# Small products on parts of the TensorE array: row tiles of 64 for the products with T and T^2, column tiles of 64 for the logits

## The chip, the cores and the metric

The kernel runs on one core of one Trainium2 chip. The metric is the device time of one execution in microseconds (us). Most executions of one kernel agree within 0.3%. Engines are named as in the profile: PE is TensorE's matmul stream, PEld its weight loads, DVE is VectorE, ACT is ScalarE, POOL is GpSimd. L880 is line 880 of that kernel's source, so the line numbers of one operation differ between kernels.

## The reference, cut to what matters

128 graphs of 64 nodes with 512 features pass four layers. Two of them are touched. All is fp32.

```python
# layer 2: attention inside a graph
weight = jnp.einsum('bqd,bkd->bqk', query, keyt)          # logits, 64 x 64 per graph
weight = adj * jnp.exp(weight)
...
# layer 3: three hops with a transition matrix T (64 x 64 per graph)
H = jnp.zeros(...)
Xk = X
for k in range(3):
    H = H + Xk @ Wk[k] + bk[k]
    Xk = jnp.einsum('bij,bjd->bid', transition, Xk)        # so X, T X and T^2 X are needed
```

## The kernel before

Two graphs make one tile of 128 tokens, and four tiles one group; there are 16 groups. Products inside a graph are done for both graphs of a tile at once, with a 128 x 128 matrix that is zero outside the two 64 x 64 blocks. So half of the multiplications are by zeros (T, T^2) or their results are thrown away (logits).

```python
# layer 3, per tile t: h (tokens x features) stationary, [T^t | (T^2)^t] moving, 256 columns
for q in range(2):
    pq = Buf("ps")
    def lm(h=h, pq=pq, t=t, q=q):
        for c in range(2):
            cc = 2 * q + c
            nc.tensor.matmul(pq.t[:, c * 2 * P:(c + 1) * 2 * P], h.t[:, cc * P:(cc + 1) * P],
                             tt.t[:, t].rearrange("p j k -> p (j k)"), start=True, stop=True)
    pe(c_mm(256, 2), lm, [h, (tt, 0), (tt, 1)], [pq])
    act(0.59, ...)                                         # copy out of PSUM
# layer 2, per emission of a quarter of the query
for o in range(2):
    for t in range(2):
        nc.tensor.matmul(quad(pl)[:, 2 * j + t, :], hT.t[:, 2 * i + o, tok(2 * j + t)], q.t[:, o, tok(t)], ...)
```

The kernel does not issue its operations in program order: a list scheduler written into it orders them by assumed costs and priorities and hands out the buffers; `pe(cost, ...)` is one indivisible operation for it. The large products are Strassen products (one helper line, L555), and they make most of the work.

## Time and profile before

The time was 2607.03 us (median of 3 runs). TensorE is busy 2562 us of the 2607. Of its 12058 matmul records, 512 are the products with T and T^2 (L880) and 512 the logits (L796); the prediction below shows their lines and works out what one costs. It calls this cost a slot: the time from the start of one matmul to the start of the next in an unbroken stream. The mean duration of a matmul on the page is longer, since matmuls overlap.

### The profile page before, as it was taken

The page shows a single profiled execution, that of the slowest core. Times are in us where ns is not written, and L with a number is a line of the kernel's source. Part 1 is how long each engine was busy: PE and PEld are TensorE (multiplying, and loading weights), DVE is VectorE, ACT ScalarE, POOL GpSimd, SP SyncE. Part 2 cuts the span into 40 slices and gives each one's busy share as a digit, 9 for nine tenths or more (in the row PEclk, how much of TensorE's full clock was granted, in tenths as well). Part 3 has the DMA queues.
Part 4 walks back from the last instruction along what each step waited for, and adds up shares of the span by engine and source line. Part 5 has one row for each costly group of instructions (what it writes and reads, how often), then busy time and mean ns, then how long its engine had stood idle before and what let it go on. Part 6 is the DMA issues. An engine that isn't in the chain of part 4 may idle for free.

```text
span 2606.9 us, 32072 instructions
## 1 busy us (share of the span) xinstructions
PE 2562.2 (98%) x12058; PEld 2047.3 (79%) x12058; DVE 1771.4 (68%) x4064; ACT 783.4 (30%) x1370; POOL 710.4 (27%) x843
## 2 busy tenths in 40 slices
PE   8999999999999999999879999999999999999999
PEld 4667777777777777767768888888888888888887
DVE  8887788788787888778675545555455564555653
ACT  2343333343333433433222212222122221222211
POOL 3323334332233433333211212122221222211220
PEclk9999999999999999999989999999999999999999
DMA  4031001011001111101220000100001000010000
GB/s 162 21 110 37 17 25 37 33 37 37 21 21 37 33 37 37 37 7 34 65 89 21 33 30 28 37 25 29 33 25 37 29 29 33 21 37 25 25 21 25
DMA packets 53355, 96.18 MB, mean 37 GB/s; under 512 B 7760, under 2 KB 7760, under 8 KB 53200
## 3 DMA queue, kind: packets, MB, share of 16 engines
q1 hardware_dynamic: 53200, 94.14, 10.8%
q8 instruction: 94, 1.54, 0.2%
q14 instruction: 61, 0.50, 0.1%
HBM read 59.52 MB, written 34.60 MB: 36 GB/s over the span
## 4 chain that ended last, share of the span: by engine, by line
PE 95%; DVE 4%; issue 0%; ACT 0%; POOL 0%; DVEq 0%; ACTq 0%; POOLq 0%
PE ps L555 58%; PE ps L773 15%; PE ps L880 4%; PE ps L502 4%; PE ps L826 2%; PE ps L796 2%; PE ps L687 2%; PE ps L675 2%; PE ps L745 1%; PE ps L871 1%; DVE st L482 1%; DVE s_s_vu_tt L547 1%; PE ps L861 1%; PE ps L709 1%; PE ps L446 1%; PE ps L592 1%
## 5 line engine op out<-in xcount | busy, mean ns | idle before, releaser
L555 PE MATMUL ps<-wb_mem,rT_a 128*128 128x256 f32 x2056 | 476.9, 380 | 1.4 <-DVE u L527 0.8
L485 POOL TENSOR_TENSOR rs<-ve,mhalf 128x1 f32<-128x1 f32 x320 | 208.1, 653 | 937.4 <-DVE ve L484 896.7
L555 PEld LDWEIGHTS ps<-wb_mem,rT_a 128*128 128x128 f32 x2056 | 386.2, 190 | 67.4 <-issue 11.2
L493 ACT ACTIVATE h<-x,nm,rs 128x512 f32<-128x512 f32 x256 | 206.6, 815 | 359.3 <-DVE nm L492 269.8
L555 PE MATMUL ps<-wb_mem,s_s_vu_tt 128*128 128x256 f32 x1152 | 276.4, 379 | 0.1
L555 PE MATMUL ps<-wb_mem,tmp_s 128*128 128x256 f32 x1152 | 263.9, 379 | 0.0
L555 PEld LDWEIGHTS ps<-wb_mem,s_s_vu_tt 128*128 128x128 f32 x1152 | 215.6, 190 | 40.7 <-issue 7.5
L555 PE MATMUL ps<-wb_mem,mT_a 128*128 128x256 f32 x1016 | 242.9, 379 | 0.0
L555 PE MATMUL ps<-wa_mem,mT_a 128*128 128x512 f32 x512 | 241.3, 596 | 0.0
L555 PEld LDWEIGHTS ps<-wb_mem,tmp_s 128*128 128x128 f32 x1152 | 215.6, 190 | 27.5
L482 DVE BATCH_NORM_STATS2 st<-x 128x6 f32<-128x512 f32 x256 | 174.4, 686 | 62.7 <-DMA x<-xm 61.2
L555 PEld LDWEIGHTS ps<-wb_mem,mT_a 128*128 128x128 f32 x1016 | 190.0, 190 | 34.0 <-issue 7.7
L583 POOL TENSOR_TENSOR u<-u,bk_b 128x256 f32<-128x256 f32 x96 | 68.3, 725 | 472.9 <-DVE u L525 347.4
L555 PE MATMUL ps<-wa_mem,s_s_vu_tt 128*128 128x512 f32 x384 | 178.3, 594 | 5.5 <-DVE s_s_vu_tt L547 5.5
L555 PEld LDWEIGHTS ps<-wa_mem,mT_a 128*128 128x128 f32 x512 | 95.9, 191 | 86.5 <-issue 82.7
L527 DVE TENSOR_TENSOR u<-ps,u 128x512 f32<-128x512 f32 (+1 forms) x160 | 84.7, 529 | 115.6 <-PE ps L555 90.5
L502 PEld LDWEIGHTS ps<-bd,h 128*128 128x128 f32 x1024 | 130.2, 195 | 32.7 <-issue 18.7
L585 DVE TENSOR_TENSOR o<-ps,u 128x256 f32<-128x256 f32 x96 | 40.7, 424 | 153.5 <-PE ps L555 149.7
L504 ACT COPY mT_a<-ps 128x512 f32<-128x512 f32 x128 | 74.7, 584 | 232.7 <-PE ps L502 160.5
L726 POOL TENSOR_TENSOR x<-x,u 128x256 f32<-128x256 f32 x96 | 70.0, 742 | 259.2 <-DVE u L525 197.4
L502 PE MATMUL ps<-bd,h 128*128 128x128 f32 x1024 | 133.2, 279 | 6.9 <-ACT h L493 4.3
L555 PEld LDWEIGHTS ps<-wa_mem,s_s_vu_tt 128*128 128x128 f32 x384 | 71.9, 190 | 86.1 <-issue 68.6
(185 smaller groups left out, 4304.6 us busy)
## 6 DMA issues: line engine op xcount, KB each, us to landing
x<-in_x_dram SPq DMA_DIRECT2D x64, 256.0 KB, 2.7
xm<-x SPq DMA_DIRECT2D x64, 256.0 KB, 2.0
x<-xm SPq DMA_DIRECT2D x64, 256.0 KB, 2.6
out_dram<-x SPq DMA_DIRECT2D x64, 256.0 KB, 2.0
adj<-in_adj_dram SPq DMA_DIRECT2D x32, 256.0 KB, 2.6
wb_mem<-in_Wk_dram SPq DMA_DIRECT2D x6, 512.0 KB, 7.1
wa_mem<-in_W1T_dram SPq DMA_DIRECT2D x2, 1024.0 KB, 8.2
wb_mem<-in_W2T_dram SPq DMA_DIRECT2D x4, 512.0 KB, 6.2
```

Of the source, the lines that this page charges most:

```text
L482: dve(0.69, lambda i=i: nc.vector.bn_stats(st.t[:, i, :], src(i)), [r[i]], [(st, i)])
L485: pool(0.57, lambda: nc.gpsimd.tensor_tensor(rs.t, ve.t, mhalf, ALU.pow), [ve], [rs])
L493: act(0.82, lambda: nc.scalar.activation(h.t, xx.t, AF.Relu, bias=nm.t, scale=rs.t), [xx, nm, rs], [h])
L502: nc.tensor.matmul(quad(p)[:, c, :], h.t[:, c * P:(c + 1) * P], rhs(), start=True, stop=True)
L504: act(0.59, lambda: nc.scalar.copy(m.t, quad(p)), [p], [m])
L527: dve(c_v(n), lambda: nc.vector.tensor_add(at(2)(), p4.t[:, :n], at(1)()), [p4, (U, 1)], [(U, 2)])
L555: nc.tensor.matmul(p.t[:, :n], lhs()[:, c, :], rhs(c), start=first and c == 0, stop=c == kc - 1, skip_group_check=True)
L583: pool(0.75, lambda: nc.gpsimd.tensor_add(U.t[:, iv], U.t[:, iu], row()[:, cols]), [u, krow], [v])
L675: nc.tensor.transpose(quad(pt)[:, c, :], z.t[:, j * D + c * P:j * D + (c + 1) * P], ident)
L726: pool(0.75, lambda: nc.gpsimd.tensor_add(xx.t[:, cols], xx.t[:, cols], U.t[:, iu]), [xx, u], [xx])
L773: nc.tensor.matmul(pair(p.t)[:, o, :], a, b, start=first and o == 0 and c == 0, stop=c == 1, skip_group_check=True)
L880: nc.tensor.matmul(pq.t[:, c * 2 * P:(c + 1) * 2 * P], h.t[:, cc * P:(cc + 1) * P], tt.t[:, t].rearrange("p j k -> p (j k)"), start=True, ...
```

## The change

The products with T and T^2 go graph by graph, on 64 of the array's 128 rows, with 128 moving columns instead of 256, alternating between the upper and the lower rows. The logits go graph by graph on 64 of its columns. How the array is cut up (whole, row halves or column halves) is called its mode below. The scheduler learns to hand out two buffers of one kind to one operation.

```diff
@@ logits, layer 2
-                        nc.tensor.matmul(quad(pl)[:, 2 * j + t, :], hT.t[:, 2 * i + o, tok(2 * j + t)], q.t[:, o, tok(t)],
-                                         start=first and o == 0 and t == 0, ...)
-            pe(c_mm(128, 4), mm, ...)
+                        for s in HALVES:
+                            at = lambda t: slice(t * P + s.start, t * P + s.stop)
+                            nc.tensor.matmul(quad(pl)[s, 2 * j + t, s], hT.t[:, 2 * i + o, at(2 * j + t)], q.t[:, o, at(t)],
+                                             start=first and o == 0 and t == 0, ...)
+            pe(c_mm(64, 4), mm, ...)
@@ products with T and T^2, layer 3 (the loop over q is gone, one operation per tile)
+                pq = [Buf("ps"), Buf("ps")]
+                def lm(h=h, pq=pq, t=t):
+                    for c in range(KD):
+                        for i, half in enumerate(HALVES):
+                            nc.tensor.matmul(quad(pq[i])[:, c, :], h.t[half, c * P:(c + 1) * P], tt.t[half, t, :, half],
+                                             start=True, stop=True)
+                pe(c_mm(128, KD), lm, [h, (tt, 0), (tt, 1)], pq)
+                for i, half in enumerate(HALVES):
+                    act(0.59, ...)                         # copy of that half's columns
+                step(0.9)
@@ cut: the scheduler counts the free buffers that an operation needs; the Strassen products wait for both copies
```

More of the change, by code (lines that the diff above doesn't have):

```diff
@@ L110, in run @@
                     t = max(o.ready, at[e])
+                    need = {}
                     for b in o.bufs:
                         if id(b) not in place:
-                            f = free[b.tag]
-                            t = max(t, min(f)[0]) if f else float("inf")
+                            need[b.tag] = need.get(b.tag, 0) + 1
+                    for tag, n in need.items():
+                        f = free[tag]
+                        t = max(t, (min(f) if n == 1 else sorted(f)[n - 1])[0] if len(f) >= n else float("inf"))
                     if t0 is None or (t, o.prio, o.seq) < (t0, pick.prio, pick.seq):
@@ L795, in mm @@
                     for t in range(2):
-                        nc.tensor.matmul(quad(pl)[:, 2 * j + t, :], hT.t[:, 2 * i + o, tok(2 * j + t)], q.t[:, o, tok(t)],
-                                         start=first and o == 0 and t == 0, stop=False, skip_group_check=True)
-            pe(c_mm(128, 4), mm, [*k[j], (q, 0), (q, 1)] if first else [*k[j], (q, 0), (q, 1), pl], [pl])
+                        for s in HALVES:
+                            at = lambda t: slice(t * P + s.start, t * P + s.stop)
+                            nc.tensor.matmul(quad(pl)[s, 2 * j + t, s], hT.t[:, 2 * i + o, at(2 * j + t)], q.t[:, o, at(t)],
+                                             start=first and o == 0 and t == 0, stop=False, skip_group_check=True)
+            pe(c_mm(64, 4), mm, [*k[j], (q, 0), (q, 1)] if first else [*k[j], (q, 0), (q, 1), pl], [pl])
             step(0.9)
@@ L873, in layer3 @@
                 act(0.59, lambda p=p, b=b: nc.scalar.copy(b.t[:, :KD, :], quad(p)), [p], [(b, 0)])
-                for q in range(2):
-                    pq = Buf("ps")
-                    def lm(h=h, pq=pq, t=t, q=q):
-                        for c in range(2):
-                            cc = 2 * q + c
-                            nc.tensor.matmul(pq.t[:, c * 2 * P:(c + 1) * 2 * P], h.t[:, cc * P:(cc + 1) * P],
-                                             tt.t[:, t].rearrange("p j k -> p (j k)"), start=True, stop=True)
-                    pe(c_mm(256, 2), lm, [h, (tt, 0), (tt, 1)], [pq])
-                    act(0.59, lambda pq=pq, b=b, q=q: nc.scalar.copy(
-                        b.t[:, KD:, :].rearrange("p (j c) k -> p c j k", j=2)[:, 2 * q:2 * q + 2],
-                        pq.t.rearrange("p (c j k) -> p c j k", c=2, j=2)), [pq], [(b, 1 + q)])
-                    step(0.9)
+                pq = [Buf("ps"), Buf("ps")]
[6 more added lines that the diff above has]
+                for i, half in enumerate(HALVES):
+                    act(0.59, lambda pq=pq, b=b, i=i, half=half: nc.scalar.copy(
+                        b.t[:, KD:, half].rearrange("p (j c) k -> p c j k", j=2),
+                        pq[i].t.rearrange("p (c j k) -> p c j k", c=KD, j=2)), [pq[i]], [(b, 1 + i)])
+                step(0.9)
                 step(0.45)
@@ L899, in layer3 @@
                 b = a3[t0 + i]
-                ak[i, 0] = [(b, 0), (b, 1)]
+                ak[i, 0] = [(b, 0), (b, 1), (b, 2)]
                 ak[i, 1] = [(b, 1), (b, 2)]
```

## The prediction

> **What bounds the kernel now.** I read the page's busy shares first, then the chain of waits, then the matmul groups kept apart by shape, and last the timeline around four places where the form of the matmul changes.
>
> ```profile
> PE 2562.2 (98%) x12058; PEld 2047.3 (79%) x12058; DVE 1771.4 (68%) x4064; ACT 783.4 (30%) x1370; POOL 710.4 (27%) x843
> ...
> PE 95%; DVE 4%; issue 0%; ACT 0%; POOL 0%; DVEq 0%; ACTq 0%; POOLq 0%
> ...
> L880 PE MATMUL ps<-s_s_vu_tt,h 128*128 128x256 f32 x512 | 120.5, 379 | 0.0
> ...
> L796 PE MATMUL ps<-y_qT,z_hT 128*128 128x128 f32 x512 | 67.4, 275 | 0.6 <-ACT y_qT L784 0.6
> ```
>
> TensorE is busy 98% of the span and makes 95% of the chain that ended last; the two groups that the change touches stood idle for 0.0 and 0.6 us in all. So the time is the sum of TensorE's slots, and whatever these groups gain or lose goes straight into the span. The mean durations (379 and 275 ns) are not the slots, since matmuls overlap; the slots come from start to start in the timeline:
>
> ```profile
> 1369.97 3.62 PE L880 MATMUL ps<-s_s_vu_tt,h 128*128 128x256 f32 x16
> 1373.43 2.75 PE L555 MATMUL ps<-wb_mem,rT_a 128*128 128x256 f32 x12
> ...
> 1293.46 1.05 PE L796 MATMUL ps<-y_qT,z_hT 128*128 128x128 f32 x8
> 1294.35 0.60 PE L773 MATMUL ps<-z_hT,wa_mem 128*128 128x256 f32 x2
> ...
> 2527.62 0.79 PE ps L613 x8
> ```
>
> Products with T and T^2: (1373.43 - 1369.97)/16 = 0.216 us an instruction, and 512 of them are 110.7 us. Logits: (1294.35 - 1293.46)/8 = 0.111 us, and 512 are 57 us. Every product in fp32 is two matmul instructions, each with its own weight load (256 products are 512 records). The last line, from the chain, is a matmul that streams a single column behind a load of 128 columns: 0.79/8 = 0.099 us a slot. So a load of 128 columns alone costs about 0.1 us, and a product with 128 moving columns, at 0.111, sits on that floor as well. A saving on moving columns below 128 is worth nothing unless the loads also get shorter or run side by side.
>
> **What the Trainium skill says.** "TensorEngine Tiling (Array Packing)", section "Key Properties", says that different tiles of the array can load weights and multiply in parallel, and that a change of tiling mode (not of tile) drains TensorE. The first half is what the change lives on; nothing in this trace shows it, since no two tiles are ever used side by side. The second half the trace does show. The setup has matmuls on 2 columns (L413) and 2 rows (L417, L418) between full-array ones:
>
> ```profile
> 36.38 1.02 PE L555 MATMUL ps<-wa_mem,s_s_vu_tt 128*128 128x512 f32 x2
> 37.34 0.59 PE L413 MATMUL ps<-wb_mem,gsc 128*2 128x512 f32 x1
> ...
> 45.55 0.27 PE L675 MATMUL ps<-ident,z_hT 128*128 128x128 f32 x1
> 45.76 1.12 PE L417 MATMUL ps<-o,tmp_s 2*128 2x512 f32 x2
> ...
> 46.72 1.02 PE L418 MATMUL ps<-o,tmp_s 2*128 2x512 f32 x2
> 47.67 0.44 PE L675 MATMUL ps<-ident,z_hT 128*128 128x128 f32 x2
> ```
>
> The line of L555 ends at 36.38 + 1.02 = 37.40, and L413 starts at 37.34, 0.06 to 0.07 before that end; L675 ends at 45.82 and L417 starts at 45.76; L418 ends at 47.74 and L675 starts at 47.67. Three times the next form begins just before the recorded end of the last one, as if it had waited for the array to run empty, whereas within one form a matmul starts a full drain earlier. Worked out: two slots of 512 columns (0.43 us each: L418's two matmuls start 46.72 and end 1.02 later, of which 0.59 is the last one) from 36.38 would have put L413 at 37.24, so it lost about 0.09 us; one slot of 0.11 (a transpose, 0.44 us for four in the chain) from 45.55 would have put L417 at 45.66, so 0.10. On top, the first weight load behind a switch is not hidden: L417's first matmul lasts 0.69 us where the later ones last 0.59, which is one load of 128 columns (0.10). A switch thus costs about 0.09 + 0.11 = 0.2 us before 128-column weights and, by the same estimate, 0.09 + 0.055 = 0.145 us before 64-column weights or a transpose (its load is short: 0.14 us of record against 0.19).
>
> "TensorE: Matmul & The Clock Gate", section "Measured speedup vs the span model", gives 3.07x for four row tiles and 2.38x for three column tiles at 512 moving columns. Those are long matmuls; it says nothing of 64 or 128 moving columns with a fresh load for each, in fp32, which is this case. The same page's section "LDWEIGHTS (loading the stationary operand)" has the load time go with the columns and not with the rows. The trace agrees for the columns (L413's loads of 2 columns last 0.085 us, those of 128 columns 0.19); for rows, the 2-row loads of L417 and L418 last 0.18, about as long as a load of 128 rows. So halving the rows of the T products does not shorten any load.
>
> **The change, part by part.**
>
> *Products with T and T^2 (64 tiles of 128 tokens, 16 groups of 4).* Removed: 4 products a tile at 256 moving columns, 8 instructions x 0.216 = 1.73 us. Added: 4 feature blocks x 2 graphs = 8 products on 64 rows, 128 moving columns, 16 instructions with 16 loads of 128 columns. If the two halves of the array work side by side, loads included, each pass takes 0.111 us per pair. The order is first half twice (two fp32 passes), second half twice, so with matmuls started in order the second half runs one slot behind: 9 slots x 0.111 = 1.0 us. Gain 0.73 x 64 = 47 us. Against it go the switches in and out of the mode, 0.2 + 0.2 us (0.145 for the way out where a transpose follows, say 0.37 for both). In the trace the L880 records come in 61 unbroken runs, 17 of which hold two whole tiles; a tile is now one operation, so I count about 50 blocks: 50 x 0.37 = 18.5 us. Net -28 us.
>
> *Logits (16 groups x 4 emissions).* Removed: 4 products of 128 x 128 with 128 moving columns, 8 x 0.111 = 0.89 us. Added: 8 products, 64 stationary and 64 moving columns, 16 instructions. Loads and streams are half as long, 0.056 us. Side by side: 9 x 0.056 = 0.50 us, gain 0.39 x 64 = 25 us. Switches: L796 stands in 63 separate runs between full-array matmuls, each with 0.145 in and 0.2 out: 22 us. Net -3 us even if all goes well.
>
> *Moved.* Copies of the products out of PSUM stay 2 x 512 elements a tile on ScalarE (0.585 us each, an engine at 30%), but a tile now needs two PSUM buffers at once and both copies before the next Strassen product may start. With TensorE fed from two groups of graphs at once, I expect that wait to be filled. The list scheduler gets other costs and one priority step fewer per tile, so the order in layers 2 and 3 shifts; TensorE idles about 45 us in all now (2606.9 - 2562.2), 10 of them in one wait at the start of the second phase, so that is worth a few us either way.
>
> Sum if tiles pair in both parts: -28 - 3 = -31 us, 2576.
>
> **Rivals.**
>
> *The loads do not pair.* One load at a time over the whole array would make the T products 16 x 0.111 = 1.78 us a tile, 0.05 more than now, plus switches: +3 + 18.5 = +21 us. The same for logits: 16 x 0.056 = 0.9 us, no gain, plus switches, +21 us. Both together 2649. For it: in the present trace loads never overlap in effect (the 0.1 us slot of one-column matmuls). Against it: the skill's statement of independent tiles; and the author's cost model counts pairs. I give pairing of row tiles two chances in three.
>
> *Issue becomes the bound.* The logits would need 32 instructions (loads and matmuls) in 0.5 us, 16 ns each. Nothing in the trace runs that fast: eight one-column matmuls with eight loads take 0.79 us, 49 ns per instruction, though the loads explain that. If 25 to 30 ns per instruction is the floor, an estimate from nothing better than that line, the logits take 0.8 to 0.96 us: no gain, and the 22 us of switches are paid, +15 to +27. The row tiles (32 instructions in 1.0 us) would just fit. I hold it as likely as the good case. Rows paired and columns not: -28 + 20 = -8, 2599.
>
> *No switch cost.* If a tile of 64 switches without draining, all of 47 + 25 = 72 us is gained, 2535, faster by 2.8%. The switches in setup speak against it.
>
> *ScalarE or PSUM becomes a wait.* With ScalarE at 30% and DVE near 55% in the second half this can only cost at the last group, where little else runs; 1 to 3 us.
>
> **Range and chances.** The four combinations are 2576 (both pair), 2599 (rows only), 2625 (columns only) and 2649 (neither). With two in three for rows and one in two for columns the mean is 0.33 x 2576 + 0.33 x 2599 + 0.17 x 2625 + 0.17 x 2649 = about 2604, and the middle of the weight lies at the first two; I lean to the median side of that, since the change was written by someone who counts on pairs, and choose 2595. An order that shifts by a few us widens the ends: 2562 to 2642. Over 2% faster means below 2555, which needs cheaper switches than the trace shows; over 2% slower means above 2659, which needs loads that are not even prefetched inside a tile mode. I give each 8%.
>
> **What would show it right or wrong.** Right: matmuls of 64*128 whose starts, over a tile, come to about 1.0 us for 16, with a gap of some 0.2 us ahead of the first one and of the matmul behind the last; the logits' 16 of 128*64 in 0.5 us (pairing) or 0.9 (not); TensorE still at 97% or more. The first phase (layers 0 and 1, up to about 1230 us) should be unchanged. Wrong: 16 row-tile instructions in 1.7 us or more; no gap at the switches; loads that start only after the matmul before them has ended; or new idle time of TensorE behind ScalarE's copies.

## The result, and the profile after

The changed kernel took 2574.98 us (median of 4 runs), against 2606.89 us for the kernel before beside it: 31.9 us less. The ratio is 0.9877, with a 95% interval of 0.986 to 0.9894. The time lies inside the range that was predicted, but the gain is 2.7 times the 12 us of the point.

The busy shares of the changed kernel, on the page:

```profile
PE 2519.7 (98%) x13082; PEld 1988.6 (77%) x13082; DVE 1798.6 (70%) x4064; ACT 786.3 (31%) x1370; POOL 713.8 (28%) x843
```

TensorE has 1024 more matmuls, and its busy time is 42.5 us shorter, while the span is 32 us shorter. It is still the bound, and it idles about 10 us more (55 us against 45). The groups by shape (engine, line, operation, output and inputs, shapes, count; busy us, mean ns; idle before):

```profile
L885 PE MATMUL ps<-s_s_vu_tt,h 64*128 64x128 f32 x1024 | 69.3, 286 | 9.4 <-ACT s_s_vu_tt L868 9.4
...
L801 PE MATMUL ps<-y_qT,z_hT 128*64 128x64 f32 x1024 | 43.8, 228 | 0.6 <-ACT y_qT L787 0.6
```

The busy time is the time in which at least one matmul of the group runs: 69.3 us where L880 had 120.5, and 43.8 where L796 had 67.4, for twice as many matmuls. Both kinds of tile do run side by side. And there is a wait that L880 didn't have, 9.4 us behind L868, the copy of T^2 out of PSUM.

The chain of waits of the changed kernel (start, length, what) shows a block of logits with its neighbours, and in a later stretch the new wait:

```profile
1454.52 1.73 PE ps L776 x8
1456.25 0.61 PE ps L801 x16
1456.86 1.92 PE ps L776 x8
...
1512.06 0.97 PE ps L866 x8
1513.03 0.02 issue
1513.06 0.59 ACT s_s_vu_tt L868
1513.65 0.04 issue
1513.69 2.98 PE ps L885 x48
```

The chain of the kernel before had the same neighbours around its logits:

```profile
2507.71 0.89 PE ps L796 x8
2508.60 2.59 PE ps L555 x12
2511.19 0.89 PE ps L796 x8
2512.08 8.63 PE ps L773 x40
```

A block of logits went from 0.89 to 0.61 us. But the eight projection matmuls behind it take 1.92 us where the same eight take 1.73 behind other products on the whole array: 0.19 us, the way out of the mode. So a block nets 0.89 - 0.61 - 0.19 = 0.09 us, and 63 blocks some 6 us.

Inside the blocks the starts say how full the array is. In a block of one tile's row tiles two matmuls start 6 or 7 ns apart, and from the second pair on the next two follow 112 ns later; in a block of logits it is 6 or 7 ns and 58 ns. Eight slots, in both, and the second slot comes late behind the first load. The timeline of one block of row tiles, matmuls alone:

```profile
1479.69 1.16 PE L885 MATMUL ps<-s_s_vu_tt,h 64*128 64x128 f32 x16
1480.79 0.70 PE L831 MATMUL ps<-s_s_vu_tt,bd 128*128 128x512 f32 x1
```

The 16 matmuls occupy 1.10 us from first start to the next operation's start, where two of the 0.86 us halves of L880 stood. The first matmul of L831 lasts 0.70 us, as L417's 0.69 did in the prediction; later ones of that shape last 0.59. That is the load that isn't hidden.

### The profile page after: what moved, and what is told of

The parts are those of the page before. It is cut to its first block, busy times and chain, and to the rows that moved or that the text cites. A ratio compares the mean times of both kernels' runs of the same rounds, so it can differ in the third digit from the quotient of the medians.

```text
span 2574.9 us, 34142 instructions
## 1 busy us (share of the span) xinstructions
PE 2519.7 (98%) x13082; PEld 1988.6 (77%) x13082; DVE 1798.6 (70%) x4064; ACT 786.3 (31%) x1370; POOL 713.8 (28%) x843
## 4 chain that ended last, share of the span: by engine, by line
PE 95%; DVE 4%; ACT 1%; issue 0%; POOL 0%; DVEq 0%; ACTq 0%; POOLq 0%
PE ps L558 59%; PE ps L776 15%; PE ps L505 4%; PE ps L885 3%; PE ps L831 2%; PE ps L690 2%; PE ps L678 2%; PE ps L801 1%; PE ps L876 1%; PE ps L748 1%; DVE st L485 1%; DVE s_s_vu_tt L550 1%; PE ps L866 1%; PE ps L595 1%; PE ps L712 1%; PE ps L449 1%
## 5 line engine op out<-in xcount | busy, mean ns | idle before, releaser
L488 POOL TENSOR_TENSOR rs<-ve,mhalf 128x1 f32<-128x1 f32 x320 | 195.6, 614 | 1136.5 <-DVE ve L487 1065.1
L586 POOL TENSOR_TENSOR u<-u,bk_b 128x256 f32<-128x256 f32 x96 | 83.8, 892 | 207.5 <-DVE u L530 98.6
L526 ACT COPY u<-ps 128x512 f32<-128x512 f32 (+1 forms) x160 | 73.3, 458 | 221.7 <-PE ps L558 120.9
L505 PE MATMUL ps<-bd,h 128*128 128x128 f32 x1024 | 133.2, 279 | 7.0 <-ACT h L496 4.3
```

The lines of the kernel that those rows point to most:

```text
L488: pool(0.57, lambda: nc.gpsimd.tensor_tensor(rs.t, ve.t, mhalf, ALU.pow), [ve], [rs])
L505: nc.tensor.matmul(quad(p)[:, c, :], h.t[:, c * P:(c + 1) * P], rhs(), start=True, stop=True)
L526: act(n / 1200 + 0.17, lambda: nc.scalar.copy(at(0)(), p1.t[:, :n]), [p1], [(U, 0)])
L586: pool(0.75, lambda: nc.gpsimd.tensor_add(U.t[:, iv], U.t[:, iu], row()[:, cols]), [u, krow], [v])
```

## The experiments

The theory after the result: (1) both kinds of tile pair fully, 8 slots a block; (2) every change of mode costs about 0.09 us before the first matmul starts, as if the array had to run empty, and one unhidden load (0.10 us for 128 columns, 0.05 for 64); (3) the new order of instructions takes part of the gain back, by the wait behind the copy of T^2. The rivals: the order makes the gain rather than costing it; the logits carry as much as the T products; switches are cheap.

### One part at a time

**e1_rows_only.** The changed kernel with the logits of the kernel before (the diff of the logits above, undone). The scheduler's assumed cost is the same for both forms, so all engines keep the changed kernel's order (both forms come to 0.888 us in its formula).

> The T products on 64 rows as in the change, the logits as before; the order of instructions on every engine is that of the changed kernel, since the schedule's costs are the same for both forms of the logits. Theory (both parts pair, a switch costs what the trace of the changed kernel shows): the logits are worth little net. In the trace of the changed kernel a block of logits takes 8 slots of 0.058 us where 8 of 0.111 stood, 0.42 us less, and pays about 0.09 + 0.05 in and 0.09 + 0.10 out, 0.34; 63 blocks give 27 - 21 = 6 us. So 2581 us, 6 above the changed kernel. Rival (the logits carry as much as the T products, about 15 us): 2590. Rival (logits lose by their switches): 2570 or less.

Measured: 2578.43 us (2577.53 to 2579.31), ratio 0.9887 (0.9871 to 0.9902). The logits are worth 3.4 us in this order, with some 4 us of uncertainty on either side.

**e2_logits_only.** The kernel before with the logits of the change; its order stays as it was.

> The logits on 64 columns alone, on the kernel before, whose order of instructions it keeps exactly. Theory: 6 us below the kernel before, 2601 us, and no other line moves. Rival (the reordering of layers 2 and 3, not the pairing, makes the gain of the changed kernel): this kernel would still show 6 us, so the test of that is the run with the changed order and full-array products. Rival (switches eat it): 2607 or above.

Measured: 2602.05 us (2601.3 to 2602.83), ratio 0.9978 (0.9966 to 0.9991): 5.4 us less than the 2607.49 beside it. The logits gain little, and they gain. The rival of 15 us falls.

**e3_new_order_full_array.** The changed kernel's operations, costs and order, with the T products as full-array matmuls again. The copies out of PSUM are adapted to it.

```diff
-                        for i, half in enumerate(HALVES):
-                            nc.tensor.matmul(quad(pq[i])[:, c, :], h.t[half, c * P:(c + 1) * P], tt.t[half, t, :, half],
-                                             start=True, stop=True)
+                        nc.tensor.matmul(pq[c // 2].t[:, c % 2 * 2 * P:(c % 2 + 1) * 2 * P], h.t[:, c * P:(c + 1) * P],
+                                         tt.t[:, t].rearrange("p j k -> p (j k)"), start=True, stop=True)
```

> The changed kernel with the T products on the full array again (4 products of 256 moving columns into the same two PSUM buffers), logits on 64 columns, and the order of instructions of the changed kernel on every engine. Theory: the row tiles pay 64 x (1.73 - 0.90) = 53 us less 34 switches in and out at 0.385 = 13 us, so 40 us, while the wait behind the copy of T^2 (9.4 us) belongs to the order and stays. So 2575 + 40 = 2615 us, above the kernel before with logits alone (2601) by the 9 to 14 us that the order costs. Rival (the order gains by itself): 2595 or less.

Measured: 2618.23 us (2617.63 to 2619.35), ratio 1.0041 (1.0029 to 1.0054), slower than the kernel before. So the row tiles in the new order are worth 2618.2 - 2575.0 = 43.2 us, and the new order alone costs 2618.2 - 2602.05 = 16.2 us. With the 5.4 of the logits the sum is 43.2 + 5.4 - 16.2 = 32.4, against 31.9 measured. That the sum fits is no check, since e3 and e2 cancel in it; it is a way of sharing out the gain. "The order" here takes in the two PSUM buffers that an operation now needs at once. Its list of waits of TensorE (what waited for what: us in total, times, longest) has the line

```profile
PE ps L884 <- ACT s_s_vu_tt L868: 9.4, 14, 0.7
```

which is the changed kernel's line to the digit and isn't in the kernel before: in the new order the transposes that could fill the time of the copy come ahead of the T^2 product, so nothing stands between that product and its use. In the kernel before, 12 Strassen matmuls stood there. The first matmul behind such a wait lasts 0.483 us instead of 0.379, its load unhidden: 14 x 0.10 = 1.4 us more. Another part of the 16 us is in the last group, where three gaps of TensorE (1.08, 0.68 and 0.67 us; e2 has one, of 0.88) follow within 5 us; the first two add 0.9 us to e2's. Below are busy times (PE, PEld, DVE, ACT, POOL), granted clock (the share of the full TensorE clock that was let through), DMA share and GB/s: two stretches of this run there, then the like of the first in e10, an experiment told below that has the same three gaps:

```profile
2562.22:2565.63 3.41, 1.65 (x11) 1.08 (x10) 2.37 (x7) 0.58 (x1) 0.00 (x0) 1.00 0.20 77
2565.63:2572.46 6.83, 6.16 (x18) 4.74 (x17) 0.00 (x0) 1.75 (x3) 0.00 (x0) 0.50 0.10 38
...
2525.38:2528.79 3.41, 1.81 (x12) 1.39 (x12) 1.77 (x4) 0.74 (x2) 0.00 (x0) 1.00 0.24 90
```

In e3 the granted clock fell to 0.50 for 6.83 us behind the first two gaps, which costs about half of the 6.16 us of matmuls there, some 3.1 us. The profile of the changed kernel has such a spell of 6.8 us at the same place, and its last block of three tiles takes 5.08 us there where the other fourteen take 2.71. Of the eight profiles with three such gaps, three fell (changed kernel, e3, e4) and five did not (e1, e5, e6, e7, e10). All changes of the clock in these traces lie on a grid of 3.41 us that runs through the profile. The stretch of the grid just before the fall held 1.76 us without a matmul in the three that fell; in this group the others had at most 1.60 in any stretch. So whether the gaps fall into one stretch seems to decide it. It is no fixed threshold: earlier in the programs, and near their ends, a few stretches with 1.75 to 2.0 us kept the full clock. For e3 this makes 9.4 + 1.4 + 0.9 + 3.1 = 14.8 of the 16.2 us, in the profiled execution; the rest is not traced.

### What a change of mode costs

**e4_double_switches.** One transpose on the full array in the middle of each block of row tiles. Its result is overwritten, so the output is right.

```diff
                     for c in range(KD):
+                        if c == 2:
+                            nc.tensor.transpose(quad(pq[0])[:, 3, :], h.t[:, :P], ident)
```

> The changed kernel with one full-array transpose (0.109 us, its result overwritten by the last product) in the middle of each of the 64 row-tile blocks: two more switches of mode for each, same order otherwise. Theory: 0.109 for itself, 0.09 + 0.05 out into a transpose, 0.09 + 0.10 back in: 0.44 us a block, 28 us in all, 2603. Rival (a switch is only dear where waits or other things fall together with it, or the transposes run beside a half): 64 x 0.109 = 7 us, 2582.

Measured: 2602.63 us (2601.37 to 2605.11), 27.7 us above the changed kernel, where 28 were expected. That is 27.7/64 = 0.43 us for one transpose of 0.109 with two switches, 0.32 us for the pair of switches. The timeline of one block agrees:

```profile
1479.92 0.72 PE L887 MATMUL ps<-s_s_vu_tt,h 64*128 64x128 f32 x8
1480.57 0.33 PE L885 MATMUL ps<-ident,h 128*128 128x128 f32 x1
1480.83 0.72 PE L887 MATMUL ps<-s_s_vu_tt,h 64*128 64x128 f32 x8
```

From the start of one half of the block to that of the other it is 0.91 us, of which four slots of 0.112 are 0.45; 0.46 us is left for the transpose and the two switches. Sixty-four transposes and the switches around them cost nearly the whole gain of the change.

### Whether neighbours must alternate

**e5_rows_not_alternating** and **e6_logits_not_alternating.** The loops exchanged, so that all matmuls of one half come before all of the other.

```diff
-                    for c in range(KD):
-                        for i, half in enumerate(HALVES):
+                    for i, half in enumerate(HALVES):
+                        for c in range(KD):
```

```diff
-                for o in range(2):
-                    for t in range(2):
-                        for s in HALVES:
+                for s in HALVES:
+                    for o in range(2):
+                        for t in range(2):
```

> The changed kernel with the two loops of a row-tile block exchanged: all 4 products of the upper 64 rows, then all 4 of the lower. Same products, same order of everything else. Theory: halves work side by side only where their matmuls stand next to each other in program order, since matmuls start in order; each half then runs alone, 16 slots of 0.112 instead of 8, +0.9 us x 64 = 57 us, 2632, which is slower than the kernel before. Rival (the queue looks far enough ahead to pair them anyway): 2575, no change.

> The same for the logits: all products of the first 64 columns, then all of the second. Theory: +0.46 us x 64 = 30 us, 2605. Rival (column tiles pair in whatever order): 2575.

Measured: 2597.97 us (2596.2 to 2598.44) for the rows and 2591.22 us (2590.9 to 2593.05) for the logits, 23 and 16 us above the changed kernel. Neither theory nor rival: the order matters, but only some 40 to 55% of the expected loss came. The chain of the first has

```profile
1480.70 1.64 PE ps L885 x16
```

1.64 us where the alternating block took 1.09. The starts in the trace tell why. The first half starts at 0, 0.213, 0.325, 0.437 and 0.548 us of the block; then, at 0.554, the second half begins, though three matmuls of the first half, earlier in program order, still wait; they run at 0.660, 0.772 and 0.883 beside the second half's. The matmul at 0.883 is the one that signals that the first half is done. From then on the second half runs alone until 1.438. In the logits it is the same: the second half begins at 0.288, behind the fifth of eight. All 19 row-tile blocks of a single tile agree within 2 ns. So in these traces TensorE looks past three waiting matmuls for one that fits an idle part of the array, and no further. The changed kernel lives on this too: a product is two records, both ahead of the other half's in program order, and yet the halves start together.

**e10_two_and_two** tests that reading: the order upper, upper, lower, lower puts four records of one half before four of the other.

```diff
-                    for c in range(KD):
+                    for c0 in (0, 2):
                         for i, half in enumerate(HALVES):
-                            nc.tensor.matmul(...)
+                            for c in (c0, c0 + 1):
+                                nc.tensor.matmul(...)
```

> The changed kernel with the row-tile products in the order upper, upper, lower, lower. Each product is two matmuls, so four matmuls of one half stand before four of the other. Theory (found in the run with the loops exchanged: a matmul of the idle half starts while up to three matmuls of the busy half, earlier in program order, still wait): the second half starts one slot late and then both keep on, 9 slots for 8; 34 blocks x 0.11 = 4 us, 2579. Rival (only direct neighbours pair): 12 slots or more a tile, 64 x 0.45 = 29 us, 2604.

Measured: 2575.68 us (2573.86 to 2576.35), so the halves pair. In the trace the single blocks take 0.991 us from the first start to the last, where the changed kernel has 0.890: one slot, as expected, but not where it was expected. The second half starts 0.014 us behind the first. The slot is lost in the middle: the second half's fifth load starts at 0.553, right behind the first half's fifth matmul (0.549), when three of that half wait, and isn't hidden, so the next matmul comes 0.206 us later instead of 0.112. This is the same reach of three. The blocks of three tiles lose 0.063 us each, so 19 x 0.10 + 15 x 0.063 = 2.9 us in all, which don't show in the time. The clock stayed at 1.00 in the last group of this profile, which the changed kernel's did not; that is worth some 3 us and may hide it.

### Fewer switches, no wait, and a better version

**e7_logits_fused.** The logits of two emissions in one operation: 32 blocks for 63.

```diff
-            first = not said
-            said.append(1)
+            said.append((i, j, q))
+            if len(said) % 2:
+                return
+            first, two = len(said) == 2, said[-2:]
             def mm():
+                for n, (i, j, q) in enumerate(two):
...                  (the products as in the change, for both)
-            pe(c_mm(64, 4), mm, ...)
+            pe(c_mm(64, 8), mm, ...)
```

> The changed kernel with the logits of two emissions in one operation: 32 blocks of 32 matmuls instead of 63 of 16, so 31 switches in and out fewer, the same number of products. Theory: 31 x 0.34 = 10.6 us less, 2564; the order shifts as well, some us either way. Rival (waiting for the second half of the query costs TensorE what the switches cost): 2575.

Measured: 2559.86 us (2558.79 to 2561.57), ratio 0.9818 (0.9806 to 0.9831): 15.1 us below the changed kernel. 31 pairs of switches at 0.34 are 10.6. The rest fits the order, though no run separates it: the wait behind the copy of T^2 has shrunk from 9.4 us to

```profile
PE ps L888 <- ACT s_s_vu_tt L871: 5.4, 8, 0.7
```

**e8_t2_in_two_copies.** T^2 is computed and copied in two halves, two tiles each, in two PSUM buffers.

```diff
-            for t in range(T):
-                nc.tensor.matmul(quad(p2)[:, t, :], tr.t[:, t, :], tt.t[:, t, 0, :], ...)
-        pe(c_mm(128, T), m2, [*trk, (tt, 0)], [p2])
-        act(0.59, lambda: nc.scalar.copy(tt.t[:, :, 1, :], quad(p2)), [p2], [(tt, 1)])
+        for n in range(2):
+            def m2(n=n):
+                for t in (2 * n, 2 * n + 1):
+                    nc.tensor.matmul(quad(p2[n])[:, t % 2, :], tr.t[:, t, :], tt.t[:, t, 0, :], ...)
+            pe(c_mm(128, 2), m2, [*trk, (tt, 0)], [p2[n]])
+            act(0.38, lambda n=n: nc.scalar.copy(tt.t[:, 2 * n:2 * n + 2, 1, :], quad(p2[n])[:, :2, :]), [p2[n]], [(tt, 1, n)])
```

> The changed kernel with T^2 computed and copied in two halves (graphs of tiles 0, 1 and of tiles 2, 3, in two PSUM buffers), so that the first row-tile block waits for a copy of 256 columns that runs beside the second half's matmuls. Theory: the wait of TensorE behind the copy of T^2 (9.4 us in all, 14 times 0.67) shrinks to about 0.3 each, 5 us gained, and the order shifts, 2566 to 2571. Rival (the wait is filled by idle elsewhere): 2575.

Measured: 2562.19 us (2560.52 to 2563.37), ratio 0.9825 (0.9812 to 0.9838): 12.8 us less. The wait is gone from the list altogether, and the last group has no spell of low clock before the very end. That makes 9.4 + 3.1 = 12.5 us. The split thus did more than expected, because it also moved the order. Its trace says that both had a part: four transposes (0.44 us) now stand between the T^2 product and the row tiles (1587.35 us in one group), and a single copy of 0.585 us from where the second half's copy starts (1587.02) would have ended 0.26 us behind that start. So, as an estimate from these figures, the order took some 0.4 us of each wait of 0.67 and the halves the rest.

**e9_fused_and_split.** Both together.

> Fused logits and T^2 in two copies together, the two that gained alone (2560 and 2562 against 2575 of the changed kernel). Theory: one saves switches, the other a wait, so they add but for the order: 2575 - 15 - 13 = 2547; part of both single gains came from the order of the list schedule, which can't be had twice, so 2547 to 2555. Rival (both only shift the same idle time of TensorE): 2560.

Measured: 2555.26 us (2552.83 to 2555.95), ratio 0.9801 (0.9787 to 0.9814). This is 19.7 us below the changed kernel, and 10.6 us of switches plus 9.4 us of wait are 20.0. The parts that both runs had in common are had once, as the upper end of the expectation said.

**e11_left_products_in_quarters.** On top of that, the products of h with the block-diagonal matrices of layers 0 and 1, in quarters of the array: 64 rows, 64 columns, four at a time.

```diff
-        p, m = Buf("ps"), Buf(tag)
+        p, m = [Buf("ps"), Buf("ps")], Buf(tag)
             for c in range(KD):
-                nc.tensor.matmul(quad(p)[:, c, :], h.t[:, c * P:(c + 1) * P], rhs(), start=True, stop=True)
-        pe(c_mm(128, KD), mm, [h, *r], [p])
-        act(0.59, lambda: nc.scalar.copy(m.t, quad(p)), [p], [m])
+                for i, half in enumerate(HALVES):
+                    for cols in HALVES:
+                        nc.tensor.matmul(quad(p[i])[cols, c, :C], h.t[half, c * P + cols.start:c * P + cols.stop], rhs()[half, half], ...)
+        pe(0.8, mm, [h, *r], p)
+        for i, half in enumerate(HALVES):
+            act(0.38, lambda i=i, half=half: nc.scalar.copy(m.t[:, :, half], quad(p[i])[:, :, :C]), [p[i]], [m])
```

> On top of fused logits and T^2 in two copies: the 128 products of h with the block-diagonal matrices of layers 0 and 1 (8 matmuls at 0.112 us, half of each multiplied by zeros) as 64 x 64 tiles, four at a time, 16 products of 64 rows, 64 columns, 64 moving columns. Theory: four tiles run at once, 8 slots of 0.058, 0.43 us less for each of 128 blocks = 55 us, less about 93 to 128 switches in and out at 0.34 = 32 to 44 us, so 11 to 23 us faster than the run with fused logits and split T^2. Rival (the queue can't feed four tiles, 64 instructions in 0.46 us, so that only two run at a time): 0.93 us a block and the switches are lost, 30 to 45 us slower than that run.

Measured: 2532.18 us (2530.05 to 2532.45), ratio 0.9714 (0.97 to 0.9727), and right. It is 23.1 us faster than e9 and 74 us faster than the kernel before. The group by shape is

```profile
L508 PE MATMUL ps<-bd,h 64*64 64x64 f32 x4096 | 87.4, 226 | 9.1 <-ACT h L497 5.8 <-DVE bd L723 2.2 <-DVE z_hT L583 1.0
```

4096 matmuls in 87.4 us of busy time, where 1024 had 133.2. In the trace a block of 32 takes 0.477 us from the first start to the last, which is seven slots of 0.058, the first load (0.05, unhidden) and 0.02 between the four of a group. So 64 instructions (matmuls and loads) pass in under half a microsecond, and in this trace issue is no bound down to about 8 ns an instruction. The blocks stand in 95 runs; 128 x 0.43 - 95 x 0.34 = 55 - 32 = 23 us, as measured.

## Why the prediction was right or wrong

*What bounds the kernel: right.* TensorE is the bound before and after, and the trace's slots carry over into the span. The first 1230 us are unchanged, as predicted (TensorE busy 1212.44 and 1212.42 us). e2, e4, e9 and e11 came within 2 us of sums of slots and switches.

*The price of a switch: right.* The prediction took 0.2 us before 128-column weights and 0.145 before 64-column weights, from three places in the setup. e4 measured 0.32 us for a pair whose way out leads into a transpose, against 0.145 + 0.2 = 0.345.

*The weighing of pairing: this is the step that failed.* The prediction gave row tiles "two chances in three" and column tiles "one in two", held "issue becomes the bound" for "as likely as the good case", and chose 2595 between outcomes of which none was 2595. Both pair fully, loads included. The rival gave a block of logits 0.8 to 0.96 us, from a floor of 25 to 30 ns an instruction; measured are 16 matmuls and 16 loads in 0.46 us from first start to last, some 14 ns an instruction, and 0.61 us for the block in the chain. Nothing in the trace of before spoke for a bound by issue: the one line it was leaned on, one-column matmuls at 49 ns an instruction, was explained by the loads, as the prediction itself said. e11 shows instructions at 8 ns. The sum for the case that came true, 2576, is within 1 us of the result, and it should have been the point. The weighing put it at a gain of 12 us where 32 came.

*That sum was right partly by luck.* Three of its terms were off and nearly cancel. First, the slot of lag ("9 slots") rested on "matmuls started in order", which e5 refutes: both halves start together, so there are 8, which is worth 64 x (0.111 + 0.056) = 10.7 us more gain. Second, "about 50 blocks" of row tiles are 34, because three tiles often stand together: 16 x 0.37 = 6 us more gain. Third, under "Moved", the wait of a tile for its copies was expected to be filled and the order to be worth "a few us either way". The order cost 16 us (e3 against e2), 9.4 of them at the copy of T^2, a wait that the prediction didn't name. The wait that it did name, of the Strassen products for a tile's copies, doesn't stand in the changed kernel's list; that one is filled.

*The logits: right.* "-3 us even if all goes well" became -3.4 to -5.4, with the eighth slot.

*The other rivals.* Loads that do not pair would have made 2649; they do pair. Switches without cost would have made 2535; e4 excludes it. A wait for ScalarE was put at 1 to 3 us in the last group alone; it came in 14 groups, for 9.4 us.

## What to carry to other kernels

Parts of the array run side by side, and each part then streams only its own columns (fewer rows alone shorten nothing here: a slot of 0.112 us on 64 rows, 0.111 on 128); but a change between the full array and its parts costs about 0.34 us for the way in and out, so the gain per block must be set against that, and blocks of one mode belong together (e7 gained 15 us from fusing, about 10.6 of it in switches). Let the halves alternate, or at most two products at a time. When one engine's work shrinks, look at what used to stand between a product and the copy that it waits for: with a list scheduler the filler may move, and here the order took back 16 of the 49 us that the matmuls gained.

## What the Trainium skill lacked or had wrong

- "TensorE: Matmul & The Clock Gate", section "The mechanism" (Part 3), says that matmuls start and end in strict program order. In e5 the second half's first three matmuls start at 0.554, 0.768 and 0.879 us of a block, each ahead of a matmul of the first half that comes earlier in the program (0.660, 0.772, 0.883). So TensorE looked past three waiting matmuls. These are recorded starts; the ends are modelled.
- "TensorEngine Tiling (Array Packing)", section "Key Properties", says that a change of mode drains TensorE and gives no number. Here a matmul behind a change starts about 0.09 us late, and its load, 0.10 us for 128 columns and 0.05 for 64, is not hidden; e4 gives 0.32 us for both ways with a transpose on the way out.
- The same page has no number for weight loads that run side by side. With a fresh load before each matmul, in fp32, pairs of row tiles keep the slot of one full-array matmul (0.112 us for two), pairs of column tiles 0.058 us for two, and quarters 0.058 us for four.
- "TensorE: Matmul & The Clock Gate", section "HAM oscillation — how this bites in real kernels", asks for no idle gaps over about 3.4 us. In e3 the granted clock fell to 0.50 for 6.83 us behind two gaps of 1.08 and 0.68 us, 1.76 us of idle time in one stretch of 3.41 us; the changed kernel and e4 did the same. In e10, with the same gaps but at most 1.60 us in a stretch, it stayed at 1.00. So short gaps that add up within a stretch can do it, though not always: elsewhere some stretches with up to 2.0 us kept the full clock.
